# A two-layer gated cross-attention kernel: where weights are inspected and where ternary weights are made

## The chip, the core and the metric

The kernel runs on one core of a Trainium2 chip. The metric is the device time of one execution in microseconds (us); the time before is the median of three executions. TensorE is called PE, VectorE DVE, ScalarE ACT, GpSimd POOL; SyncE (SP) issues most of the DMAs.

## What is computed

Eight sequences of 100 tokens with 512 features pass through two layers. Each layer attends to a context of 722 rows and then applies a feed-forward network; both are added to the tokens through a tanh gate. Reduced to what matters:

```python
x = x + tanh(g_xattn[0]) * attn0(layernorm(x), ctx, ctx, mask)     # 16 heads of 32
x = x + tanh(g_ffn[0])   * ffn0(layernorm(x))
x = x + tanh(g_xattn[1]) * (attn1(layernorm(x), ctx, ctx) @ Wo.T + bo)
x = x + tanh(g_ffn[1])   * ffn1(layernorm(x))

# ffn0: w1, w2 [2048,512], h1, h2 [2048,2048], w3 [512,2048] drawn from -1, 0, 1; one scale a row
h = silu(x @ w1.T * s1) * (x @ w2.T * s2)
h = gelu(h @ h1.T * t1);  h = gelu(h @ h2.T * t2);  y = h @ w3.T * s3

# ffn1: weights are made ternary, activations are rounded to 8 bits
wq = clip(round(w / mean(abs(w))), -1, 1) * mean(abs(w))
aq(x) = clip(round(x * 127 / max(abs(x))), -128, 127) * max(abs(x)) / 127
y = (silu(aq(x) @ gate_q.T) * (aq(x) @ up_q.T)) -> aq -> @ down_q.T
```

## The kernel before

`flow` (line 45 onward) writes the whole program once, and every engine executes its instructions in the order in which they are written (`ORDERED`, line 21). SP's list is its DMAs: one that has to wait holds all SP DMAs behind it. `flow` is written twice: a short path that splits activations of the first feed-forward into two parts, hi and lo, in the fp32r format (the weights then have to be exact in it), and a general path that runs only if the inspected weights were not. `verdict` holds the outcome. With these inputs the short path alone runs.

**First attention.** `attention` (237) runs 8 batches of 4 units; a unit (b, oc) is four heads. In a unit, PE makes scores of the first half of the keys, then of the second half; DVE adds the mask and takes maxima; ACT makes exponentials. After the second half the hook `between0` (820) is called, then `settle` (360) finishes the unit before: six turns (PE transposes of probabilities into two PSUM buffers, evicted in turn by DVE and ACT to pT), then the product with the values. Between these pieces `take` pulls matmuls from a filler: the k and v projections of the next batch (`projections`, 156), whose k is evicted by ACT and whose v by DVE. A batch's filler runs in the order k, v, k, v, about one to a unit. At the start of a batch `load_ctx` (150) orders the first part of the context two batches ahead, in the middle the second part; three buffers hold parts. At oc = 1 `mask_bias` (786) orders the next batch's mask from SP and converts it on DVE.

`between0` also advances `inspections` (539) three times a call. A step loads 128x1024 weights by a POOL DMA; POOL takes the low 16 bits of each and adds them up. There are 88 steps.

**First feed-forward** (`feed_forward`, 463). It is run in two halves of 400 tokens (`hf` 0 and 1). There are 8 blocks of w1 and w2, 16 of h1, 16 of h2 and 4 of w3, each 1 MB and 32 matmuls. `block` (426) orders one by a POOL DMA into the pool `wts`, which has four 1 MB buffers for all large weights; a buffer is held until its last reader in program order. After a block come gelu and hi on ACT and lo on DVE (`split`, 431). In half 0, layer h1 carries `mean_weights` (578): twelve 1 MB loads of w_gate, w_up and w_down on SP and 24 Abs on ACT with accumulated sums, from which come a mean and its inverse. Layer h2 carries side work: in half 0 the normalisation and transposition of the second tokens, in half 1 the queries of the second attention (`second_queries`, 881), which load wq and keep it for the second attention. Both call `ln_rstd` (109), which has POOL raise to the power -0.5 (line 115). In half 1, `make_room` (888) orders ctxT, wk and wv ahead of w3. A w3 tile holds 128 output columns and comes by four DMAs of 256 KB.

**Second attention** (hook `between1`, 961). The same units, without a mask. `quantise_weights` (602) advances once a call: a 1 MB load on SP, then on POOL multiply and add, subtract and max with -1, min with 1, and a cast to fp8. The last batch's filler is the second feed-forward for batches 0 to 6: `hidden_rows`, `quantised_hidden` (694; on POOL, line 705 multiply and add, line 706 subtract and min) and `down_rows`; batch 7 follows with DVE in POOL's place.

Of the kernel before, what the change touches and what calls it, by code (L numbers as in the profile page):

```python
# [9 lines left out]
F32 = mybir.dt.float32  # L10
# [33 lines left out]
def flow(tc: tile.TileContext, a: dict, out: bass.AP, verdict):  # L44
# [378 lines left out]
    WT = F32R if short else F32  # L423
    COST = TH / 2400 * (1 if short else 4) + 0.016

    def block(src, shape, name):
        w = wts.tile(shape, WT, tag="w", name=name)
        nc.gpsimd.dma_start(w, src)  # L428
        return w

# [32 lines left out]
    def feed_forward(hf, xs, sets, early_work, side_work, before_down, after_down):  # L463

        everything = slice(0, TH)
# [8 lines left out]
        for op in range(HC // 2):  # L474
            w = block(a["w12"][op], [P, 2, 2, KC, P], "w12")
# [20 lines left out]
        for layer, m in enumerate(("h1", "h2")):  # L496
            outs = []
            for oc in range(HC):
                w = block(a[m + "_w"][oc], [P, HC, P], m)
# [9 lines left out]
                next((early_work, side_work)[layer], None)  # L509
                yield COST  # L510
            h = outs
            for _ in (early_work, side_work)[layer]:
                pass
# [3 lines left out]
        for oc in range(KC):  # L517
            w = wts.tile([P, HC // KC, KC, P], WT, tag="w", name="w3")
            for q in range(HC // KC):
                nc.gpsimd.dma_start(w[:, q], a["w3_w"][q][:, :, oc * P : (oc + 1) * P])  # L520
            acc = ps_sc.tile([P, 512], F32, tag="sc", name="ps_w3")
            yield from product(acc, w.rearrange("p q c o -> p (q c) o"), h)
            nc.scalar.activation(yT[oc], acc[:, :TH], AF.Identity, scale=s3g[:, oc : oc + 1])
            yield COST
        after_down()
        for i in range(BH):
            pt = ps_t.tile([P, 512], F32, tag="pst", name="ps_y")
            for oc in range(KC):
                nc.tensor.transpose(
                    pt[:S, oc * P : (oc + 1) * P], yT[oc][:, i * S : (i + 1) * S], ident  # L530
                )
            yield 0.34
            b = hf * BH + i
            nc.vector.tensor_add(x[:, b, :], x[:, b, :], pt[:S, :])
            ln_stats(b)
# [3 lines left out]
    def inspections():  # L539
        blocks = [a["w12"][i].rearrange("p a b c d -> p (a b c d)") for i in range(HC // 2)]  # L540
        blocks += [a[m][i].rearrange("p a b -> p (a b)") for m in ("h1_w", "h2_w") for i in range(HC)]
        blocks += [a["w3_w"][i].rearrange("p a b -> p (a b)") for i in range(HC // KC)]
        n = HID // 2
        blocks = [src[:, h * n : (h + 1) * n] for src in blocks for h in range(2)]
        home = rooms["seen"]
        seen = home.tile([P, n], I32, tag="seen", name="seen")
        part = home.tile([P, n], I32, tag="part", name="part")
        nc.gpsimd.memset(seen, 0)

        def fetch(src):  # L550
            w = home.tile([P, n], F32, tag="w_seen", name="w_seen", bufs=2)
            nc.gpsimd.dma_start(w, src)
            return w

        w_next = fetch(blocks[0])
        for i in range(len(blocks)):
            w = w_next
            if i + 1 < len(blocks):
                w_next = fetch(blocks[i + 1])
            low = w.bitcast(U16).rearrange("p (n two) -> p n two", two=2)[:, :, 0]  # L560
            nc.gpsimd.tensor_copy(part, low)  # L561
            nc.gpsimd.tensor_tensor(seen, seen, part, ALU.add)  # L562
            yield
        worst = small.tile([P, 1], F32, tag="worst", name="worst")
        nc.vector.reduce_max(worst, seen, axis=AX.X)
        pt = ps_t.tile([P, 512], F32, tag="pst", name="ps_seen")
        nc.tensor.transpose(pt[:1, :P], worst, ident)
        most = small.tile([1, 1], F32, tag="most", name="most")
        nc.vector.reduce_max(most, pt[:1, :P], axis=AX.X)
        nc.vector.tensor_scalar_min(verdict, most, 1.0)  # L570
        yield

# [3 lines left out]
    def mean_weights():  # L578

        for name in ("w_gate", "w_up", "w_down"):  # L580
            sums8 = small.tile([P, 8], F32, tag="w_sums", name="w_sums")
            for q in range(4):
                w = weights(a[name][q], [P, HID], name)
                yield
                for h in range(2):
                    cols = slice(h * HID // 2, (h + 1) * HID // 2)
                    i = 2 * q + h
                    nc.scalar.activation(
                        w[:, cols], w[:, cols], AF.Abs, accum_out=sums8[:, i : i + 1]
                    )  # L590
            yield
            row = small.tile([P, 1], F32, tag="w_row", name="w_row")
            nc.vector.reduce_sum(row, sums8, axis=AX.X)
# [6 lines left out]
            quant[name] = mean, inv  # L600

    def quantise_weights():

        for name in ("w_gate", "w_up", "w_down"):
            wq = rooms["q"].tile([P, 4, HID], FP8, tag=name, name=name + "_q")
            quant[name] += (wq,)
            for q in range(4):
# [481 lines left out]
```

## Time and profile before

| what | value |
|---|---|
| median of three executions | 1929.3 us (1926.24 to 1939.88) |
| the profiled execution, its time | 1932.18 us |
| its span, first to last instruction | 1930.4 us |
| first attention's batches begin (ctxT DMA behind the previous filler) | 93.3, 152.4, 216.1, 280.3, 344.8, 413.1, 475.6 us |
| first feed-forward, half 0 and half 1, to the second attention | from 621 us, to about 1240 us |
| mean granted PE clock | 0.962 |
| DMA | 204.78 MB, mean 106 GB/s |

In the page, busy times are shares of the span, and a row of 40 digits shows each engine's busy tenths in 40 slices of 48 us. In the timeline a row gives start, duration, engine, line, operation, output<-input and count, and in brackets the idle time ahead of it with what ended it. A record of SPq is a DMA issue. Matmul durations overlap: the distance of starts (0.181 us for 400 columns) is the rate.

### The profile page before, as it was taken

What the parts mean: (1) busy time and instruction counts of PE and PEld (TensorE: products, weight loads), DVE (VectorE), ACT (ScalarE), POOL (GpSimd) and SP (SyncE); (2) the same over time, 40 slices, a digit from 0 to 9 for tenths busy, and PEclk for the clock granted to TensorE, in tenths of its full rate; (3) what the DMA queues carried; (4) which work ended last, traced back from release to release, by engine and by line L of the source; (5) the groups of instructions that cost most, each with busy time, mean ns of one, the idle gap of its engine ahead of it and who ended that gap; (6) DMA issues with size and microseconds to landing.
All of it is one profiled execution on the core that took longest, in us unless ns stands there. A gap on an engine that the chain in (4) does not pass through costs nothing. (4 is left out here: it accounts for less than half of the span.)

```text
span 1930.4 us, 27472 instructions
## 1 busy us (share of the span) xinstructions
PE 1758.0 (91%) x11227; PEld 1209.7 (63%) x11227; DVE 772.7 (40%) x2180; ACT 586.1 (30%) x1187; POOL 683.7 (35%) x459
## 2 busy tenths in 40 slices
PE   5999999999979998799999896799999999998785
PEld 2555555555545988799999896655555545554453
DVE  2345455545554400110410110244444455456664
ACT  0043333343334343221322111033433333433431
POOL 0689999970030000102000001147767600003143
PEclk8999999999999998899999998899999999998898
DMA  4354454441021467457555445411122101000000
GB/s 150 128 181 158 143 168 145 144 135 38 16 77 45 168 247 261 153 175 178 170 176 175 140 144 149 103 59 61 59 83 75 54 15 32 1 1 1 9 10 19
DMA packets 67039, 204.78 MB, mean 106 GB/s; under 512 B 6408, under 2 KB 39176, under 8 KB 52340
## 3 DMA queue, kind: packets, MB, share of 16 engines
q0 software_dynamic: 41088, 138.42, 22.5%
q1 hardware_dynamic: 25816, 64.51, 10.1%
q8 instruction: 90, 1.47, 0.3%
q14 instruction: 45, 0.37, 0.1%
HBM read 201.28 MB, written 1.64 MB: 105 GB/s over the span
## 5 line engine op out<-in xcount | busy, mean ns | idle before, releaser
L453 PE MATMUL ps_h<-hi,h 128*128 128x400 f32 x1024 | 363.3, 355 | 27.0 <-DMA h<-in_h_w 27.0
L191 PE MATMUL ps_v<-wv,ctxT 128*128 128x512 f32 (+1 forms) x768 | 387.2, 612 | 0.0
L171 PE MATMUL ps_k<-ctxT,wk 128*128 128x338 f32 (+1 forms) x1024 | 364.1, 483 | 22.6 <-ACT kT L179 14.8
L453 PE MATMUL ps_h<-lo,h 128*128 128x400 f32 x1024 | 360.1, 352 | 0.0
L275 ACT ACTIVATE p<-p,negm 100x722 f32<-100x722 f32 x256 | 229.4, 896 | 244.5 <-DVE negm L272 243.8
L290 PEld LDWEIGHTS ps_pT<-ident,p 100*128 100x128 f32 (+1 forms) x1536 | 169.6, 139 | 192.4 <-issue 76.6
L171 PEld LDWEIGHTS ps_k<-ctxT,wk 128*128 128x128 f32 x1024 | 179.3, 193 | 124.0 <-issue 37.0
L290 PE MATMUL ps_pT<-ident,p 100*128 100x100 f32 (+1 forms) x1536 | 197.6, 253 | 43.2 <-DVE pT L293 21.3
L453 PEld LDWEIGHTS ps_h<-hi,h 128*128 128x128 f32 x1024 | 197.9, 193 | 29.5 <-DMA h<-in_h_w 22.1
L562 POOL TENSOR_TENSOR seen<-seen,part 128x1024 int32<-128x1024 int32 x88 | 209.4, 2379 | 7.5
L434 DVE TENSOR_TENSOR lo<-g,hi 128x400 fp32r<-128x400 f32 x96 | 55.3, 576 | 389.1 <-ACT hi L433 389.1
L453 PEld LDWEIGHTS ps_h<-lo,h 128*128 128x128 f32 x1024 | 197.8, 193 | 0.7
L191 PEld LDWEIGHTS ps_v<-wv,ctxT 128*128 128x128 f32 (+1 forms) x768 | 123.5, 186 | 97.7 <-issue 93.9
L179 ACT ACTIVATE kT<-ps_k,bk 128x384 f32<-128x384 f32 (+1 forms) x128 | 71.8, 562 | 320.2 <-PE ps_k L171 318.3
L293 DVE COPY pT<-ps_pT 128x400 f32<-128x400 f32 x180 | 102.6, 572 | 165.2 <-PE ps_pT L290 165.0
L428 POOL DMA_DIRECT2D h<-in_h_w x64 | 34.0, 532 | 360.1 <-PE ps_h L453 297.5
L115 POOL TENSOR_TENSOR ln_r<-ln_v,root 100x1 f32<-100x1 f32 (+1 forms) x14 | 10.7, 762 | 411.0 <-DVE ln_v L113 411.0
L258 DVE CUSTOM_DVE_ANT_0 p<-sc,mask 100x361 f32<-100x361 f32 x256 | 121.4, 530 | 64.0 <-PE sc L249 64.0
L258 DVE CUSTOM_DVE_ANT_0 p<-sc,zero 100x361 f32<-100x361 f32 x256 | 121.7, 530 | 57.9 <-PE sc L249 57.7
L295 ACT COPY pT<-ps_pT 128x400 f32<-128x400 f32 (+1 forms) x204 | 99.0, 487 | 113.0 <-PE ps_pT L290 112.5
L503 ACT ACTIVATE g<-ps_h,h_s 128x400 f32<-128x400 f32 x64 | 38.0, 594 | 313.3 <-PE ps_h L453 313.3
L561 POOL CAST part<-w_seen 128x1024 int32<-128x1024 uint16 x88 | 92.0, 1046 | 20.9 <-DMA w_seen<-in_h_w 12.0
(166 smaller groups left out, 2079.8 us busy)
## 6 DMA issues: line engine op xcount, KB each, us to landing
h<-in_h_w POOLq DMA_DIRECT2D x64, 1024.0 KB, 5.1
w_seen<-in_h_w POOLq DMA_DIRECT2D x64, 512.0 KB, 3.8
w<-in_w POOLq DMA_DIRECT2D x16, 1024.0 KB, 5.1
ctxT<-in_ctxT SPq DMA_DIRECT2D x16, 768.0 KB
ctxT<-in_ctxT SPq DMA_DIRECT2D x16, 676.0 KB
w_seen<-in_w POOLq DMA_DIRECT2D x16, 512.0 KB, 3.9
w_gate<-in_w_gate SPq DMA_DIRECT2D x8, 1024.0 KB
w_up<-in_w_up SPq DMA_DIRECT2D x8, 1024.0 KB
```

What stands on the lines that cost most here:

```text
L171: nc.tensor.matmul(ps[:, :kn], wk[:, c, oc * P : (oc + 1) * P], cT[:, c, :kn], start=(c == 0), stop=(c == KC - 1),)
L179: nc.scalar.activation(kT[:, oc, k0 : k0 + kn], ps[:, :kn], AF.Identity, bias=bk[:, oc : oc + 1],)
L191: nc.tensor.matmul(ps[:rn, :], cT[:, c, r0 - k0 : r0 - k0 + rn], wv[:, c, :], start=(c == 0), stop=(c == KC - 1),)
L258: nc.vector.tensor_tensor_reduce(ps[j][:, cols], sc[j][:S, :HALF], bias[:, cols], 1.0, LOWEST, ALU.add, ALU.max, m2[:, j, h : h + 1],)
L275: nc.scalar.activation(ps[j], ps[j], AF.Exp, bias=negm[:, j : j + 1], accum_out=sums[:, 4 * oc + j : 4 * oc + j + 1],)
L290: nc.tensor.transpose(pt[:kn, j, :], ps[j][:, k0 : k0 + kn], ident[:S, :S])
L293: nc.vector.tensor_copy(sb[:kn], pt[:kn])
L295: nc.scalar.copy(sb[:kn], pt[:kn])
L434: nc.vector.tensor_sub(two[1][:, cols], src, two[0][:, cols].bitcast(F32))
L453: nc.tensor.matmul(acc[:, :TH], w[:, c, :], part, start=(c == 0 and k == 0), stop=(c == len(ins) - 1 and k == len(two) - 1),)
L561: nc.gpsimd.tensor_copy(part, low)
L562: nc.gpsimd.tensor_tensor(seen, seen, part, ALU.add)
```

## The change

1. `inspections` is gone. In half 0 of the first feed-forward, `block` loads a raw copy by SP, POOL copies it to fp32r, and DVE ORs the raw bits into `seen` in four instructions of 512 columns. `judge` masks the low 12 bits after the half and sets `verdict`. Half 1 loads as before.
2. `mean_weights` is gone. `quantise_weights` runs in the first attention, six steps to a call of `between0`. Its data come in 72 stages of 128x342 (24 to a matrix), twice: once for Abs on ACT, once for the four POOL operations, after which SP stores the fp8 stage to DRAM. Two buffers hold stages. At (6, 3) what is left of it is drained. The second attention loads the three results at (0, 0) (`fetch_quantised`).
3. w3 comes in four blocks of 512 input rows, each contiguous, into four PSUM accumulators at once.
4. wq of the second attention is dropped after its first use and loaded again after the first feed-forward; wv is ordered after w3.
5. `quantised_hidden` no longer clips at 127 in its second operation.

```diff
+    LOOKS = 4
...
-    def block(src, shape, name):
-        w = wts.tile(shape, WT, tag="w", name=name)
-        nc.gpsimd.dma_start(w, src)
+    def block(src, shape, name, seen):
+
+
+        if seen is None:
+            w = wts.tile(shape, WT, tag="w", name=name)
+            nc.gpsimd.dma_start(w, src)
+            return w
+        raw = wts.tile(shape, F32, tag="w", name=name)
+        nc.sync.dma_start(raw, src)
+        w = wts.tile(shape, F32R, tag="w", name=name + "_r")
+        axes = " ".join("abcd"[: len(shape) - 1])
+        flat = f"p {axes} -> p ({axes})"
+        nc.gpsimd.tensor_copy(w.rearrange(flat), raw.rearrange(flat))
+        bits = raw.bitcast(I32).rearrange(flat)
+        n = HID // LOOKS
+        for i in range(LOOKS):
+            nc.vector.tensor_tensor(seen, seen, bits[:, i * n : (i + 1) * n], ALU.bitwise_or)
         return w
+
+    def judge(seen):
+
+        nc.vector.tensor_scalar(seen, seen, 0xFFF, None, ALU.bitwise_and)
+        worst = small.tile([P, 1], F32, tag="worst", name="worst")
+        nc.vector.reduce_max(worst, seen, axis=AX.X)
+        pt = ps_t.tile([P, 512], F32, tag="pst", name="ps_seen")
+        nc.tensor.transpose(pt[:1, :P], worst, ident)
+        most = small.tile([1, 1], F32, tag="most", name="most")
+        nc.vector.reduce_max(most, pt[:1, :P], axis=AX.X)
+        nc.vector.tensor_scalar_min(verdict, most, 1.0)
 
...
+        seen = None
+        if short and hf == 0:
+            seen = sets[0](0).tile([P, HID // LOOKS], I32, tag="seen", name="seen")
+            nc.vector.memset(seen, 0)
...
-            w = block(a["w12"][op], [P, 2, 2, KC, P], "w12")
+            w = block(a["w12"][op], [P, 2, 2, KC, P], "w12", seen)
...
-                next((early_work, side_work)[layer], None)
+                if layer == 1:
+                    next(side_work, None)
                 yield COST
-            for _ in (early_work, side_work)[layer]:
-                pass
+        for _ in side_work:
+            pass
...
-        for oc in range(KC):
-            w = wts.tile([P, HC // KC, KC, P], WT, tag="w", name="w3")
-            for q in range(HC // KC):
-                nc.gpsimd.dma_start(w[:, q], a["w3_w"][q][:, :, oc * P : (oc + 1) * P])
-            acc = ps_sc.tile([P, 512], F32, tag="sc", name="ps_w3")
-            yield from product(acc, w.rearrange("p q c o -> p (q c) o"), h)
-            nc.scalar.activation(yT[oc], acc[:, :TH], AF.Identity, scale=s3g[:, oc : oc + 1])
-            yield COST
+        acc = [ps_sc.tile([P, 512], F32, tag="sc", name="ps_w3") for _ in range(KC)]
+        for q in range(HC // KC):
+            w = block(a["w3_w"][q], [P, KC, D], "w3", seen)
+            for oc in range(KC):
+                cols = slice(oc * P, (oc + 1) * P)
+                for c in range(KC):
+                    for k, part in enumerate(h[q * KC + c]):
+                        first = q == 0 and c == 0 and k == 0
+                        last = q * KC + c == HC - 1 and k == len(h[0]) - 1
+                        nc.tensor.matmul(
+                            acc[oc][:, :TH], w[:, c, cols], part, start=first, stop=last
+                        )
+                        yield COST
+                if q == HC // KC - 1:
+                    nc.scalar.activation(
+                        yT[oc], acc[oc][:, :TH], AF.Identity, scale=s3g[:, oc : oc + 1]
+                    )
         after_down()
+        if seen is not None:
+            judge(seen)
...
-    def inspections():
...
-            low = w.bitcast(U16).rearrange("p (n two) -> p n two", two=2)[:, :, 0]
-            nc.gpsimd.tensor_copy(part, low)
-            nc.gpsimd.tensor_tensor(seen, seen, part, ALU.add)
-            yield
...
-    def mean_weights():
-
...
+    STAGE = 342
+
+    def stages(name):
+
+        where = [(q, c0, min(STAGE, HID - c0)) for q in range(4) for c0 in range(0, HID, STAGE)]
+
+        def fetch(i):
+            q, c0, n = where[i]
+            t = xts.tile([P, STAGE], F32, tag=f"xc{i % 2}", name="w_stage")
+            nc.sync.dma_start(t[:, :n], a[name][q][:, c0 : c0 + n])
+            return t[:, :n], i, q, slice(c0, c0 + n)
+
+        coming = fetch(0)
+        for i in range(len(where)):
+            now = coming
+            if i + 1 < len(where):
+                coming = fetch(i + 1)
+            yield now
+
...
+    def quantise_weights():
+
+
+        for name in NAMES:
+            n = 4 * -(-HID // STAGE)
+            sums = small.tile([P, n], F32, tag="w_sums", name="w_sums")
+            for w, i, q, cols in stages(name):
+                nc.scalar.activation(w, w, AF.Abs, accum_out=sums[:, i : i + 1])
                 yield
-                for h in range(2):
-                    cols = slice(h * HID // 2, (h + 1) * HID // 2)
-                    i = 2 * q + h
-                    nc.scalar.activation(
-                        w[:, cols], w[:, cols], AF.Abs, accum_out=sums8[:, i : i + 1]
-                    )
             row = small.tile([P, 1], F32, tag="w_row", name="w_row")
...
-    def quantise_weights():
-
-        for name in ("w_gate", "w_up", "w_down"):
...
-            for q in range(4):
-                w = weights(a[name][q], [P, HID], name)
-                yield
-                nc.gpsimd.tensor_scalar(w, w, quant[name][1], MAGIC, ALU.mult, ALU.add)
-                nc.gpsimd.tensor_scalar(w, w, MAGIC, -1.0, ALU.subtract, ALU.max)
-                nc.gpsimd.tensor_scalar_min(w, w, 1.0)
-                nc.gpsimd.tensor_copy(wq[:, q, :], w, saturate=False)
-
-        mg, mu, md = (quant[name][0] for name in ("w_gate", "w_up", "w_down"))
+            wq = dram.tile([P, 4, HID], FP8, tag=name, name=name + "_dram")
+            quant[name] = mean, inv, wq
+
...
+        for name in NAMES:
+            _, inv, wq = quant[name]
+            for w, i, q, cols in stages(name):
+                nc.gpsimd.tensor_scalar(w, w, inv, MAGIC, ALU.mult, ALU.add)
+                nc.gpsimd.tensor_scalar(w, w, MAGIC, -1.0, ALU.subtract, ALU.max)
+                nc.gpsimd.tensor_scalar_min(w, w, 1.0)
+                t = xts.tile([P, STAGE], FP8, tag=f"xc{2 + i % 2}", name="wq_stage")
+                t = t[:, : cols.stop - cols.start]
+                nc.gpsimd.tensor_copy(t, w, saturate=False)
+                nc.sync.dma_start(wq[:, q, cols], t)
+                yield
+
+    def fetch_quantised():
+        for name in NAMES:
+            t = rooms["q"].tile([P, 4, HID], FP8, tag=name, name=name + "_q")
+            nc.sync.dma_start(t, quant[name][2])
+            quant[name] = quant[name][:2] + (t,)
...
-        engine.tensor_scalar(hq, h, MAGIC, 127.0, ALU.subtract, ALU.min)
+        engine.tensor_scalar(hq, h, MAGIC, None, ALU.subtract)
...
-        for _ in range(3):
-            next(inspected, None)
+        for _ in range(6):
+            next(quantised, None)
         if oc == 1 and b + 1 < B:
...
         if (b, oc) == (B - 2, KC - 1):
+            for _ in quantised:
+                pass
...
-        second["q"] = wq, bq
+        second["bq"] = bq
...
         second["wk"] = weights(a["L1_Wk"], [P, KC, D], "wk1")
+
+    def make_more_room():
         second["wv"] = weights(a["L1_Wv"], [P, KC, D], "wv1")
-
-    def make_more_room():
...
+    second["wq"] = weights(a["L1_Wq"], [P, KC, D], "wq1")
     wo = weights(a["L1_Wo"], [P, KC, D], "wo1")
...
-            for _ in queries(1, *second["q"], turned_room(), second["qT"][1]):
+            for _ in queries(1, second["wq"], second["bq"], turned_room(), second["qT"][1]):
                 take(0.7)
             output_bias()
+            fetch_quantised()
             return
-        next(quantised, None)
```

## The prediction

> **What bounds the kernel now.** I read the page's busy shares and slices first. TensorE (PE) is busy 91% of the span. GpSimd (POOL) is full in slices 2 to 8, the first attention, where it inspects weights.
>
> ```profile
> PE 1758.0 (91%) x11227; PEld 1209.7 (63%) x11227; DVE 772.7 (40%) x2180; ACT 586.1 (30%) x1187; POOL 683.7 (35%) x459
> PE   5999999999979998799999896799999999998785
> POOL 0689999970030000102000001147767600003143
> ```
>
> So a cost matters where it stops PE, and a gain is only what PE waits for today. The PE timeline gives those waits. The worst are at the end of the second feed-forward half, where w3 tiles come through one buffer:
>
> ```profile
> 1194.30 0.67 PE L453 MATMUL ps_w<-hi,w 128*128 128x400 f32 x1 [11.98 <-DMA w<-in_w_w]
> 1206.75 0.45 PE L453 MATMUL ps_w<-hi,w 128*128 128x400 f32 x1 [3.67 <-DMA w<-in_w_w]
> 1218.04 0.70 PE L453 MATMUL ps_w<-hi,w 128*128 128x400 f32 x1 [3.63 <-DMA w<-in_w_w]
> 1230.55 0.45 PE L453 MATMUL ps_w<-hi,w 128*128 128x400 f32 x1 [3.62 <-DMA w<-in_w_w]
> ```
>
> An attention batch takes 62.5 us while POOL is idle (413.7 to 476.2 us) and 64.6 while it inspects (280.8 to 345.4). The feed-forward runs 32 matmuls to a block in 5.81 us (the spacing of POOL's block DMAs).
>
> **Gains.** (1) w3. Before, wq, wk and wv hold three of the four weight buffers; after, wq is dropped and reloaded and wv loads later, so three buffers serve w3, in contiguous blocks. The waits above sum to 22.9 us. From 1194.30 to the first ps_y at 1238.05 is 43.75 us; less three waits 32.9, where four blocks should take 23.3: 9.6 us lost to a slow clock after each wait (granted 0.66 to 0.84 there). Of 32.5 I count **-31**.
>
> (2) The first half's stalls. Without the means' 12 MB and sums on the way, PE loses waits of 2.8 + 3.0 + 2.9 us for h blocks and 1.9 + 2.0 + 2.0 for the mean's row: 14.6. At 805 PE waits 10.2 us, since POOL's DMA issues stand behind its pow (ln_r, L115). That block's first 17 matmuls then come 0.333 us apart rather than 0.181: 2.6 more. After, the loads go through SP, and only POOL's copy stands behind the pow: pow 1.0, copy 1.9, DVE's lead 2.2, about 5 left of 12.8. Sum 14.6 + 7.8, rounded down: **-20**. The same stall in the second half (8.2 us at 1080) stays.
>
> (3) The tail. The clip at 127 goes from hq on POOL:
>
> ```profile
> 1804.14 7.08 POOL L706 TENSOR_SCALAR hq<-hid 100x2048 bf16<-100x2048 f32 x1
> 1811.30 0.56 POOL L115 TENSOR_TENSOR ln_r<-ln_v,root 100x1 f32<-100x1 f32 x1
> 1817.26 1.52 PE L249 MATMUL sc<-kT,xa 32*100 32x361 f32 x2 [8.16 <-DVE m L258]
> 1911.03 1.51 PE L716 MATMUL ps_hq<-ident_bf,hq 100*128 100x100 bf16 x16 [9.00 <-POOLq L1017]
> ```
>
> A lone subtract has no row. Multiply and add takes 1.97 us, a lone min 5.37: bounds 1.9 and 5.4; I take 1.97, as it too has no min. That is 5.1 us off each. PE waits for it twice (through the pow at 1811, and directly at 1911), and once POOL holds up L352 (3.67 us against 0.75): **-11** (-3 at 5.4). (4) No inspection: 2.1 us for each of batches 0 to 2; batches 3 to 5 have POOL busy again: **-6**. The second attention has PE full while POOL quantises (1280 to 1480): freeing POOL there is 0. Gains: 68.
>
> **Costs in the first attention, phase A.** The means are now 72 stages of 128x342 (175 KB), six at each call of the hook, calls 1 to 12 (batches 0 to 2). Each is an Abs on ACT, which waits for its SP DMA through two buffers. Abs of 1024 took 1.05 us and 0.19 for the accumulator; I take 0.5 + 0.19. Landing: 1 MB took 5.1 us, 512 KB 3.8, so a line gives 2.9 for 175 KB. A rule of the Trainium skill bears on it (DMA: Bandwidth & Descriptors, section "Anatomy of one DMA": some 2.0 us fixed, plus the size over 436 GB/s): 2.4. Two stages have landed when a group starts; each further pair waits for a buffer, an issue and a landing, 3.7 us from start to start. Six take 0.69 x 2 + 2 waits of 3 us + 0.69 x 2 = about 8.8 us of ACT's time (7.8 by the rule; 6 us less in all). Behind them on ACT stand exponentials and pT copies, and PE turns wait for these:
>
> ```profile
> 159.56 0.58 ACT L179 ACTIVATE kT<-ps_k,bk 128x384 f32<-128x384 f32 x1 [2.99 <-PE ps_k L171]
> 160.18 0.90 ACT L275 ACTIVATE p<-p,negm 100x722 f32<-100x722 f32 x1
> 161.62 0.49 ACT L295 COPY pT<-ps_pT 128x400 f32<-128x400 f32 x1 [0.45 <-PE ps_pT L290]
> ```
>
> The group falls between the first two lines. ACT is free at 160.1, so the group ends at 168.9, the exponential at 170.0, the pT copy at 170.5. PE's fourth turn needs that buffer and came at 163.7: 6.8 us. That holds in units filled with k projections (ACT evicts up to the hook), two of four per batch. In v units ACT has nothing for some 9 us before the hook, which hides the group; there the mask's DMA comes about 1 us late. Three batches: 6 x 6.8 + 3, and half of the 2.6 us restart each: **+52** (20 to 65).
>
> **Phase B.** Stages 0 to 71 of quantising run in batches 3 to 5: four POOL operations, then a store. At 2048 columns they take:
>
> ```profile
> 1275.58 1.98 POOL L610 TENSOR_SCALAR w_gate<-w_gate,w_gate_i 128x2048 f32<-128x2048 f32 x1 [24.45 <-issue]
> 1277.65 7.09 POOL L611 TENSOR_SCALAR w_gate<-w_gate 128x2048 f32<-128x2048 f32 x1
> 1284.83 5.37 POOL L612 TENSOR_SCALAR w_gate<-w_gate 128x2048 f32<-128x2048 f32 x1
> 1290.26 1.89 POOL L613 CAST w_gate_q<-w_gate 128x2048 fp8e4<-128x2048 f32 x1
> ```
>
> 16.3 us over 6 is 2.7; about 0.15 fixed per operation and gaps of 0.08 add 0.8: **3.5 us** a stage (3.2 to 3.8), 252 in all. The Trainium skill (GPSIMD Engine Reference, section 4.1 "Engine selection") calls one-input elementwise work on GpSimd roughly line-rate. By it all four would cost as the cast, 0.42 us each: 1.8 with gaps, and phase B would hide. The rows with max and min, at 7.09 and 5.37, speak against it; I use the rows.
>
> POOL itself keeps nobody waiting, but SP does. SP issues in program order: the store waits for POOL's cast, and the next batch's mask stands behind twelve stores. SP is held to PE anyway:
>
> ```profile
> 280.26 0.54 SPq L153 DMA_DIRECT2D ctxT<-in_ctxT  x1
> 280.85 0.54 SPq L791 DMA_DIRECT2D mask<-in_mask  x1
> ```
>
> The ctxT load waits for the end of a batch's projections (S); today the mask follows at once, and DVE casts it 25.6 us later (153.0 against 178.0 for batch 1). After, in batch 3: two issues and a landing (3.5) + 12 x 3.5 + 2.9 = 48.4 after S. DVE stands 22.8 us at the cast; behind it are the evictions of turns and so PE, which runs on for 3 us at most: 20. Then SP waits at the second ctxT load, 33.4 us after S, which slips with PE; POOL runs dry there for about 8 us. So a batch takes 24 x 3.5 + 8 = 92 us in place of 64: 28 in each of batches 4 and 5. The mask of batch 7 is in time, 25 us into batch 6. Sum **+76** (40 to 95). What would be late next, ctxT, has half a batch of slack.
>
> **Costs in the first feed-forward half.** A block is now loaded raw by SP, copied by POOL, ORed into `seen` by DVE, and holds two of four buffers. The loop: after block i-1 ends, gelu, hi and lo take 1.9 us (DVE reaches the ORs behind lo), four ORs of 512 at 0.69 + 0.03 (L329's undisturbed duration) 2.9, then SP loads block i+2 (5.2 from issue to use, as for w_gate at 1270.40), POOL copies 1.9, with 0.3 of semaphores: 12.2 us against two blocks, 11.6. So 0.3 a block x 44 = 13; I take **+12**. If the copy meets the ORs (L329 reached 2.0 beside a busy POOL), up to 1.3 a block, 57; if the DMA lands in 4.5, 0. judge() puts a mask, a maximum and a transpose ahead of ps_y: **+2**.
>
> **Edits at nothing.** The second attention's hook now issues three 1 MB loads of ternary weights on SP at (0, 0), ahead of the next ctxT: the first reader of the weights is batch 7's filler, and ctxT has half a batch (31 us) to come; without that cover some 15 us, once. The reloaded wq gets the buffer of w3's third block, lands 5.2 us later while the fourth (5.8) still runs, and is read after it; without that cover 5. wv stands behind w3's second block, 11.6 us ahead of the end. The twelve 1 MB loads that leave the second attention kept only POOL waiting, and the 24 Abs that leave the first feed-forward half ran on an ACT that waits for PE there. On the DMA engines 44 MB of inspection (share 0.46 in a batch) give way to 24 MB of stages and 3 MB of stores.
>
> **Sum.** -31 - 20 - 11 - 6 + 52 + 76 + 12 + 2 = +74. The profiled span is 1930.4 us (1932.2 with what lies around it), 3 us above the median of 1929.3; so 2004 to 2006 for the profiled run and **2003** for the median.
>
> **Rivals.** *POOL keeps up* (not slower): if a stage takes 1.85 us or less, twelve come before DVE reaches the mask (3.5 + 12 x 1.85 + 2.9 = 28.6, the 25.6 and 3 us of PE's run-ahead). Then phase B is 0: 1927; if ACT's groups are also half hidden, 1900. For it: the rule above, and POOL off the critical path today. Against: rows L611, L612. *Contention in the feed-forward*: ORs and copies collide, +45 more: 2048. For it: L329 and L352 stretch beside POOL; against: a longer period pulls them apart. *w3 still starves*, the freed buffers going elsewhere: +31, 2034. Against: wq's last reader comes seven blocks earlier.
>
> **Chances.** My case 0.58, POOL keeps up 0.24 (half of it by over 1% faster), contention 0.13, w3 starves 0.05. My case with its bounds spans 1950 to 2040. With the others the range is 1905 to 2055. A measurement here tells about 1% from no change: faster by over 1% 0.13, within 1% 0.14, slower 0.73.
>
> **What would show it.** Right: SP standing on POOL's cast in batches 3 to 5, DVE idle some 20 us before the mask's cast, those batches near 90 us; ACT idle inside Abs groups; w3 without waits; hq near 2 us. Wrong: POOL stages under 2.5 us, masks issued ahead of stores, or feed-forward blocks above 6.3 us.

## The result and the profile after

The changed kernel takes **2084.2 us** (median of four, 2080.9 to 2090.7) where the kernel before takes 1932.7 in the same rounds: a ratio of 1.079 (95% interval 1.074 to 1.084). The prediction, 2003 us with a range of 1905 to 2055, had the direction, and missed the size by 81 us. The profiled span is 2082.4 us, 152.0 above that of before.

Against the predicted sum of +74, by stages, between the same events in both traces (the x += of each batch's end, L352; the first w12 matmul; the first ps_y of each half):

| stretch | predicted | measured |
|---|---|---|
| batches 0 to 2 (phase A, less the inspection) | +46 | +73 |
| batches 3 to 5 (phase B) | +76 | +124 |
| batches 6 and 7 | 0 | -9 |
| first feed-forward, half 0 (-20 + 12 + 2) | -6 | +5 |
| half 1 (w3) | -31 | -34 |
| second attention and tail | -11 | -7 |
| sum | +74 | +152 |

The page of the changed kernel gives the same picture: PE's busy share falls from 91% to 85%, and the holes lie in the first attention's slices.

```profile
PE 1774.3 (85%) x11227; PEld 1207.4 (58%) x11227; DVE 915.4 (44%) x2358; ACT 594.9 (29%) x1283; POOL 424.6 (20%) x410
PE   5968888491927998898999998999999999998786
POOL 0000001778676201233231000000000000001222
PEclk8978999795968999999999999999999999998898
```

In slices 8, 10 and 12, PE has 4, 1 and 2 tenths. DVE's timeline of the changed kernel says what it stood at: the first three lines are the mask's cast in batches 3 to 5, with the idle time ahead of it, and the fourth is PE's next turn behind the first of them.

```profile
407.90 0.54 DVE L821 CAST mask<-mask 100x722 f32<-100x722 int32 x1 [28.27 <-DMA mask<-in_mask]
519.77 0.54 DVE L821 CAST mask<-mask 100x722 f32<-100x722 int32 x1 [46.80 <-DMA mask<-in_mask]
633.80 0.54 DVE L821 CAST mask<-mask 100x722 f32<-100x722 int32 x1 [48.58 <-DMA mask<-in_mask]
410.55 0.93 PE L290 MATMUL ps_pT<-ident,p 100*128 100x100 f32 x4 [28.02 <-DVE pT L293]
```

Before, the cast in batch 3 did not wait:

```profile
307.33 0.72 DVE L792 CAST mask<-mask 100x722 f32<-100x722 int32 x1
```

DVE's three waits sum to 123.7 us, all of phase B's loss. PE waited 28.02 us behind the first of them: the 3 us of run-ahead that the prediction gave PE did not exist. SP's queue in batch 3 shows what holds the mask, and what comes behind it (lines left out are marked `...`):

```profile
352.90 0.55 SPq L153 DMA_DIRECT2D ctxT<-in_ctxT  x1
353.55 1.05 SPq L593 DMA_DIRECT2D w_stage<-in_w_gate  x2
362.12 0.33 SPq L643 DMA_DIRECT2D w_gate_dram<-wq_stage  x1
...
403.88 0.33 SPq L643 DMA_DIRECT2D w_gate_dram<-wq_stage  x1
404.30 0.32 SPq L820 DMA_DIRECT2D mask<-in_mask  x1
417.17 0.56 SPq L153 DMA_DIRECT2D ctxT<-in_ctxT  x1
```

The mask goes out behind the twelfth store, 51.4 us after the batch began (3.5 + 12 x 3.5 = 45.5 by the prediction's numbers). Then SP stands for 12.9 us at the next ctxT load, since PE, released by this very mask, has not yet reached the middle of the batch. POOL's stages were predicted well (3.5 us): below is one line for each of the four operations of the first stage, and the next stage starts 3.70 us after it.

```profile
358.38 0.57 POOL L637 TENSOR_SCALAR w_stage<-w_stage,w_gate_i 128x342 f32<-128x342 f32 x1 [294.55 <-DMA w_stage<-in_w_gate]
359.03 1.37 POOL L638 TENSOR_SCALAR w_stage<-w_stage 128x342 f32<-128x342 f32 x1
360.49 1.07 POOL L639 TENSOR_SCALAR w_stage<-w_stage 128x342 f32<-128x342 f32 x1
361.63 0.47 POOL L642 CAST wq_stage<-w_stage 128x342 fp8e4<-128x342 f32 x1
362.08 0.56 POOL L637 TENSOR_SCALAR w_stage<-w_stage,w_gate_i 128x342 f32<-128x342 f32 x1
```

In phase A, ACT's timeline of the first group of six Abs (the filler's k eviction ahead of it, an exponential behind it) has the predicted shape: two landings in the middle, 7.4 us in all where 8.8 were predicted. A stage ordered at 100.25 is used at 102.76, one ordered at 112.12 at 115.35: 2.5 and 3.2 us, about the line's 2.9. The 2.4 that the prediction drew from the Trainium skill (DMA: Bandwidth & Descriptors, section "Anatomy of one DMA") is near, but that section gives its fit for DMAs ordered from GpSimd, and these come from SP.

```profile
99.17 0.58 ACT L179 ACTIVATE kT<-ps_k,bk 128x384 f32<-128x384 f32 x1 [2.99 <-PE ps_k L171]
99.65 0.48 ACT L615 ACTIVATE w_stage<-w_stage 128x342 f32<-128x342 f32 x1
...
102.76 0.49 ACT L615 ACTIVATE w_stage<-w_stage 128x342 f32<-128x342 f32 x1 [2.07 <-DMA w_stage<-in_w_gate]
...
106.13 0.49 ACT L615 ACTIVATE w_stage<-w_stage 128x342 f32<-128x342 f32 x1 [2.32 <-DMA w_stage<-in_w_gate]
...
107.08 0.88 ACT L275 ACTIVATE p<-p,negm 100x722 f32<-100x722 f32 x1
```

The windows view prices phase A (batches 0 to 2: length, busy time of each engine, granted clock, DMA share, GB/s). The first line is the changed kernel:

```profile
92.90:352.90 260.00, 207.57 (x1275) 112.49 (x1275) 92.65 (x291) 105.85 (x294) 0.00 (x0) 0.88 0.26 74
```

and this one the kernel before:

```profile
93.30:280.30 187.00, 181.52 (x1279) 99.15 (x1280) 97.96 (x288) 70.64 (x150) 172.63 (x132) 1.00 0.48 158
```

Of the 73 us more, PE is busy for 26 more with the same matmuls: the granted clock is 0.88 where it was 1.00. The other 47 are idle, and PE's own list of waits in that stretch says behind what. After:

```profile
PE ps_pT L290 <- ACT pT L295: 39.7, 9, 9.4
PE ps_pT L290 <- DVE pT L293: 8.3, 3, 2.9
PE ps_v L191 <- ACT kT L179: 4.1, 1, 4.1
```

Before:

```profile
PE ps_pT L290 <- ACT pT L295: 4.2, 2, 2.7
PE ps_pT L290 <- DVE pT L293: 1.3, 2, 0.9
```

So 39.6 us more are spent behind ACT, where the groups of Abs stand, and 7.0 more behind DVE. DVE itself stood 22.8 us at three masks there (16.89, 2.81 and 3.13), but most of that did not reach PE.

The tail's waits shrank little, from 8.16 to 6.33 us and from 9.00 to 7.28, since the subtract alone still takes 5.36 us:

```profile
1958.27 5.36 POOL L737 TENSOR_SCALAR hq<-hid 100x2048 bf16<-100x2048 f32 x1
1969.56 1.52 PE L249 MATMUL sc<-kT,xa 32*100 32x361 f32 x2 [6.33 <-DVE m L258]
2063.94 1.51 PE L747 MATMUL ps_hq<-ident_bf,hq 100*128 100x100 bf16 x16 [7.28 <-POOLq L1043]
```

PE's list of waits has no load of w3 in the second half any more (22.9 us before).

### The profile page after: what moved, and what is told of

It reads as the page before. It is cut to its first block, busy times and chain, and to the rows that moved or that the text cites. A ratio compares the mean times of both kernels' runs of the same rounds, so it can differ in the third digit from the quotient of the medians.

```text
span 2082.4 us, 28129 instructions
## 1 busy us (share of the span) xinstructions
PE 1774.3 (85%) x11227; PEld 1207.4 (58%) x11227; DVE 915.4 (44%) x2358; ACT 594.9 (29%) x1283; POOL 424.6 (20%) x410
## 5 line engine op out<-in xcount | busy, mean ns | idle before, releaser
L191 PE MATMUL ps_v<-wv,ctxT 128*128 128x512 f32 (+1 forms) x768 | 397.9, 626 | 4.1 <-ACT kT L179 4.1
L171 PE MATMUL ps_k<-ctxT,wk 128*128 128x338 f32 (+1 forms) x1024 | 371.5, 491 | 22.8 <-ACT kT L179 15.0
L290 PE MATMUL ps_pT<-ident,p 100*128 100x100 f32 (+1 forms) x1536 | 207.9, 262 | 194.6 <-DVE pT L293 142.0
L479 PE MATMUL ps_h<-hi,h_r 128*128 128x400 f32 x512 | 180.0, 352 | 21.6 <-POOL h_r L439 21.6
L479 PE MATMUL ps_h<-hi,h 128*128 128x400 f32 x512 | 180.2, 352 | 8.2 <-DMA h<-in_h_w 8.2
L479 PE MATMUL ps_h<-lo,h 128*128 128x400 f32 x512 | 178.1, 348 | 0.0
L479 PE MATMUL ps_h<-lo,h_r 128*128 128x400 f32 x512 | 177.9, 347 | 0.0
L443 DVE TENSOR_TENSOR seen<-seen,h 128x512 int32<-128x512 int32 x128 | 115.7, 904 | 3.3
L479 PEld LDWEIGHTS ps_h<-hi,h_r 128*128 128x128 f32 x512 | 97.3, 190 | 27.0 <-POOL h_r L439 27.0
L479 PEld LDWEIGHTS ps_h<-hi,h 128*128 128x128 f32 x512 | 97.3, 190 | 9.1 <-DMA h<-in_h_w 8.5
```

Of the source, the lines that this page charges most:

```text
L171: nc.tensor.matmul(ps[:, :kn], wk[:, c, oc * P : (oc + 1) * P], cT[:, c, :kn], start=(c == 0), stop=(c == KC - 1),)
L191: nc.tensor.matmul(ps[:rn, :], cT[:, c, r0 - k0 : r0 - k0 + rn], wv[:, c, :], start=(c == 0), stop=(c == KC - 1),)
L290: nc.tensor.transpose(pt[:kn, j, :], ps[j][:, k0 : k0 + kn], ident[:S, :S])
L443: nc.vector.tensor_tensor(seen, seen, bits[:, i * n : (i + 1) * n], ALU.bitwise_or)
L479: nc.tensor.matmul(acc[:, :TH], w[:, c, :], part, start=(c == 0 and k == 0), stop=(c == len(ins) - 1 and k == len(two) - 1),)
```

## The experiments

The theory after the result: the weights' work is short enough to be hidden, and nearly all of its 197 us in the first attention comes from *order*: the mask and ctxT behind stores on SP, Abs in groups ahead of pT copies on ACT. The rivals: the work itself is too much (POOL's long operations, DMA traffic), or it slows its neighbours through shared resources. For e1 to e4 the time is that of one execution, beside one of 1925.2 us for the kernel before; for the others it is the median of four, beside 1931 to 1934 us.

**e1: the mask ahead of the stages.** Only the mask's DMA moves, to the call before.

```diff
+        if oc == 0 and b + 1 < B:
+            later["mask"] = mask_load(b + 1)
         for _ in range(6):
             next(quantised, None)
         if oc == 1 and b + 1 < B:
-            biases[b + 1] = mask_bias(b + 1)
+            biases[b + 1] = mask_bias(b + 1, later["mask"])
```

> The changed kernel, with the next mask's DMA ordered at oc = 0 ahead of that call's six stages (its conversion on DVE stays at oc = 1). Nothing is left out. Order theory (the first attention's loss in batches 3 to 5 is the mask standing behind stores on SP, seen as DVE waits of 28, 47 and 49 us): the wait of batch 3 vanishes, and those of batches 4 and 5 shrink, because SP itself reaches a batch's start only every 24 x 3.64 us + 6 = 93 us while PE needs 64: waits of about 7, 30 and 29 us at the conversions in batches 4, 5 and 6, 66 in place of 124; the mask waits of 17 + 3 + 3 us in batches 0 to 2 go too. Time about 2015 us. Rival (POOL's work and the small transfers slow PE, ACT and DVE by contention, and the mask waits are only where the lag shows): PE gets no further, the lag shows up at another wait, and the time stays within 15 us of 2084.

Measured 2037.2 us. Phase A fell by 15 (its mask waits went), batch 3 has no wait and takes 62.5 us, but batches 4 to 6 wait 19.6, 36.4 and 38.7 us, 94.7 in all:

```profile
DVE mask L824 <- DMA mask<-in_mask: 94.7, 3, 38.7
```

As the theory said, SP arrives late at the batch's beginning itself, so a mask ordered there is late too: the wait isn't removed but comes one batch later. It is longer than the 66 us expected, since SP begins its batches 100 to 104 us apart, not 93.

**e2: shorter stages.** The subtract with max and the min make way for one multiply and add; the clip of the ternary weights to -1 and 1 is left out.

```diff
-                nc.gpsimd.tensor_scalar(w, w, MAGIC, -1.0, ALU.subtract, ALU.max)
-                nc.gpsimd.tensor_scalar_min(w, w, 1.0)
+                nc.gpsimd.tensor_scalar(w, w, 1.0, -MAGIC, ALU.mult, ALU.add)
```

> The changed kernel with POOL's two clipping operations (subtract and max, min) replaced by one multiply and add; the clipping of the ternary weights to -1 and 1 is left out. POOL work for a stage falls from 3.46 to 1.6 us, DMAs and SP order unchanged. Order theory: SP's distance between stores is then set by the store, the next fetch and its landing, about 5.6 us for two stages, 2.8 each rather than 3.64, so the masks are 12 x 0.84 = 10 us earlier in batch 3 and a batch takes about 92 us rather than 112: mask waits near 17, 28 and 28 us, 73 in place of 124; time about 2033 us. If only POOL's rate counted (no landing in the loop), stages of 1.9 us and waits under 5 us each: 1970. Rival (contention by transfers): no change beyond 15 us, since the transfers stay.

Measured 2009.9 us; the mask waits of batches 3 to 5 are 13.7, 16.8 and 20.9, 51.4 in all (73 expected). L638 takes 0.48 us where the two operations took 2.44. So the stage's length does set the wait, and the operations with max and min make most of that length. Whether a clip can be had for less was not tried.

**e3: one step after each turn.** The six steps are spread over settle's six turns.

```diff
             for c in range(NK):
                 got.append(turn(ps0, c, vector))
                 take(0.74)
+                if layer == 0:
+                    next(quantised, None)
...
-        for _ in range(6):
-            next(quantised, None)
```

> The changed kernel with the six steps of a call taken one after each of the six turns of settle, not in one group ahead of it. Nothing is left out. Theory for batches 0 to 2 (+73 us over the kernel before): ACT stands in a group of six Abs with two landings inside, ahead of the copies that PE's turns wait for, and PE's clock drops after each wait (PE busy 208 us for 182 us of work). With single steps no Abs should wait much over 1 us: batches 0 to 2 fall by about 50 us. The mask at oc = 1 then stands behind six stages fewer, so batch 3's wait falls to about 3 us and the next two to about 30 each: 64 in place of 124. Together about 1975 us. Rival (it is the amount of ACT work and of transfers): batches 0 to 2 stay within 15 us of what they took.

Measured 2000.1 us. Phase A's loss went from 73 to 14 us, as the x += of batch 2 shows (316.3 us; 375.4 with the groups; 302.4 before): 59 where 50 were expected, for the same 72 Abs. ACT's waits for stages fell from 66 to 16 us, PE's waits in phase A from 52.4 to 12.5, and PE's granted clock there was 0.97. Phase B gave back some of it, with 94.5 us of mask waits where 64 were expected.

**e4: no ORs.** The inspection's four ORs are left out.

> The changed kernel without the four ORs of a block: the inspection of the weights is left out (raw load by SP and POOL's copy to fp32r stay). First feed-forward half, 303.7 us in the changed kernel. Theory (the loop lo, four ORs, load of the block after next, copy sets the pace, 6.6 us a block on average against 5.81, and ORs beside a copy stretch from 0.69 to over 2 us): without ORs the raw buffer is free at the copy's end, blocks come every 5.81 us, the half takes about 275 us: 2055 us in all. Rival (POOL's copy and the two-deep buffers alone set the pace): the half stays above 295 us.

Measured 2052.9 us, 31 less; half 0 took 270 us in place of 304. So the ORs cost about 31 us; without them PE waits for POOL's copies only once, 4.9 us. That the ORs alone are at fault does not follow, since e12 keeps them.

**e5: w3 and wq alone**, on the kernel before (parts 3 and 4 of the change). **e6: with it hq** as two operations:

```diff
-        engine.tensor_scalar(hq, h, MAGIC, 127.0, ALU.subtract, ALU.min)
+        engine.tensor_scalar(hq, h, 1.0, -MAGIC, ALU.mult, ALU.add)
```

**e7: with both, the variance add early.** `ln_rstd` is cut in two: DVE's add of the variance is issued at h1's block 8, POOL's pow stays at the start of h2.

```diff
-        for later["xs"] in normalised(1, HI_LO[1]):
+        v = ln_var(BH, B)
+        yield
+        for later["xs"] in normalised(1, HI_LO[1], v):
...
+                if (layer, oc) == (0, 8):
+                    next(side_work)
```

> The kernel before with parts 3 and 4 alone: w3 in four blocks of rows, wq loaded again after the first feed-forward, wv ordered after w3. Theory (the gain of the second half is the w3 stalls alone, and it does not depend on the moved inspection): first matmul of the half to first sc falls by about 33 us, 1932 to about 1899. Rival (part of the 34 us came from POOL and the DMA engines being free of other parts of the change, or the reloaded wq is late without them): a gain of 20 or less, 1912 or more.

> The run with w3 by rows, and hq made on POOL as multiply by 1 and add -MAGIC (two operations, without the clip at 127, as in the change) in place of a lone subtract. Theory (POOL's price goes by the operation: multiply and add 1.97 us, lone subtract 5.36, subtract and min 7.08): hq takes about 1.97 us, both waits of the tail (8.2 and 9.0 us) shrink by about 5, and the time falls by 11 to 14 us, to about 1886. Rival (a second operation always costs, so that only the missing min counts): hq stays at 5.4 and the gain is about 7, 1892.

> The run with w3 and hq, and the variance add for the tokens turned in layer h2 issued on DVE 8 blocks of h1 earlier, so that POOL's pow does not wait on DVE's queue and POOL's DMA issues behind it go out in time. Theory (in both halves PE's stalls at the start of h2, 10.2 and 8.2 us with about 2.6 us of slow clock behind each, come from POOL's issues standing behind the pow): about 20 us less, to about 1865. Rival (the stalls come from the loads themselves being late): no change, about 1886.

Measured 1899.7, 1886.4 and 1861.1 us beside 1933.6 for before: ratios 0.983 (0.979 to 0.986), 0.976 (0.972 to 0.979) and 0.964 (0.960 to 0.969). All three theories hold. In e6, hq takes 1.90 us on POOL:

```profile
L715 POOL TENSOR_SCALAR hq<-hid x7: 1897/1897/1898, 1723.1 to 1862.3; 100x2048 bf16<-100x2048 f32 x7
```

So for 2048 columns multiply and add took 1.90 us, a lone subtract 5.36, and subtract with min 7.08. In e7, PE's waits for h loads fall from e6's 26.7 us to 8.5, and the slow clock behind the two long ones goes with them.

**e8: all masks early.** Six buffers, all masks ordered in batches 0 to 2; stages as in the change.

```diff
-    masks = pool(left, "masks", 2)
+    masks = pool(left, "masks", 6)
...
+    AHEAD = {(0, 0): 2, (0, 1): 3, (0, 2): 4, (1, 2): 5, (2, 0): 6, (2, 2): 7}
...
+        if (b, oc) in AHEAD:
+            mask_load(AHEAD[b, oc])
```

> The changed kernel with all masks ordered from SP in batches 0 to 2 into six buffers, so that no mask stands behind stores in batches 3 to 5; the conversions stay where they are. Theory (phase B costs 124 us only because the mask's DMA stands behind twelve stores on SP; the next thing late is ctxT in batches 5 and 6, since 72 stages of 3.64 us are 262 us against three batches of 64): mask waits 0, about 20 us of ctxT waits and 6 us from POOL beside DVE, 2084 to about 1985. Rival (POOL's work slows the first attention by itself, through shared SBUF access or the DMA of stages): batches 3 to 5 stay above 75 us each, 2020 or more.

Measured 1993.0 us, ratio 1.031 (1.028 to 1.035). No mask wait is left, and batches 3 and 4, in which nothing waits, take 62.5 us with POOL busy for 87 and 82% of them (x += at 358.81, 421.37, 483.78), as fast as one with POOL idle before. That refutes the rival: in these batches POOL's work and its DMAs cost nothing that shows. What remains in batches 5 and 6 is order again: twice ctxT behind stores, seen at PE (34.5 us, where 20 were expected), and once the tokens' pow behind POOL's last stages, seen at DVE.

```profile
543.97 6.40 PE L171 MATMUL ps_k<-ctxT,wk 128*128 128x384 f32 x12 [17.17 <-DMA ctxT<-in_ctxT]
596.36 4.78 PE L171 MATMUL ps_k<-ctxT,wk 128*128 128x338 f32 x10 [17.37 <-DMA ctxT<-in_ctxT]
```

```profile
640.11 0.16 DVE L117 TENSOR_TENSOR ln_u<-ln_r 100x4 f32<-100x4 f32 x1 [20.06 <-POOL ln_r L115]
```

The pow's wait was not foreseen: the stages end at 639.1, behind the point at which the program wants the first feed-forward's tokens.

**e9: the work where it is covered.** Spread as in e3, masks early, hq as in e6, and the two halves of the work interleaved, so that POOL has three stages (10.9 us) in a unit of 15.6, in buffers of their own.

```diff
+        yield from means("w_gate")
+        for step, mean_of in (("w_gate", "w_up"), ("w_up", "w_down")):
+            made = ternary(step)
+            for _ in means(mean_of):
+                yield
+                next(made)
+                yield
...
+        yield from ternary("w_down")
```

**e10: with the variance early**, as in e7. **e11: as e10, no inspection** in half 0.

> The changed kernel with the first attention's work put where it is covered: one step after each of settle's turns as in e3, w_gate's quantising interleaved with w_up's means and w_up's with w_down's (three POOL stages and three Abs to a unit, own buffers for POOL's raw stages), masks early as in e8, hq as multiply and add. POOL then has 3 stages of 3.64 us, 10.9 us, in a unit of 15.6. Theory (both phases cost only through order and crowding, the work itself fits): phase B 124 becomes 0, phase A 73 becomes about 15, hq -7, so 2084 to about 1895. Rival (SP in order: each Abs load now stands behind a store that waits for POOL, and ACT waits for it in front of pT copies): 48 Abs at 1 us and more, 1935 or above.

> The interleaved kernel with the variance add 8 blocks earlier in both halves. Theory (the stall at the start of h2 comes from what stands behind POOL's pow; in half 0 the copies, in half 1 the block loads): about 11 us in half 1 and 4 to 7 in half 0, so 15 to 18 us less than e9, near 1880. Rival (in half 0 the copies are late anyway through the ORs): 10 to 11 less, near 1885.

> The same without the inspection in the first feed-forward: half 0 loads its blocks as half 1 does, with no raw copy, no POOL copy and no OR; what the kernel would check of the weights is left out. Theory (the ORs, stretched beside POOL's copy, set the pace of half 0, as leaving them out gave 33 us): about 33 us less than e10, near 1847, and no better than the before kernel with the w3, hq and variance edits (1861) by more than its own 14 us of mean and inspection waits. Rival (with the pow out of the way the copies and ORs fit in the block time): 10 us or less.

Measured 1892.1, 1880.4 and 1848.8 us: ratios 0.979 (0.975 to 0.982), 0.973 (0.970 to 0.977) and 0.957 (0.954 to 0.961). In e9 the eighth batch's x += is at 650.1 us where before has 636.3 and the changed kernel 827.7: 191 us of loss have become 14, with every one of the 144 steps still done. e9 makes all the changes of order at once; what interleaving gives alone was not tried. e10 gives 12 us by the medians where 15 to 18 were expected, nearer to its rival's 10 to 11. In the traces half 0 (the memset of `seen` to the first ps_y) falls from 303.1 to 296.9 us and half 1 (first ps_y to first ps_y) from 283.7 to 273.4, 16 together, as the theory had it; but that is one pair of executions, and e9's was the slowest of its four. e11 puts the inspection at 32 us.

**e12: the copy on ACT.** In half 0 the raw block is copied by ACT in place of POOL, and ordered one block ahead.

```diff
-        nc.gpsimd.tensor_copy(w.rearrange(flat), raw.rearrange(flat))
+        nc.scalar.copy(w.rearrange(flat), raw.rearrange(flat))
...
+            while order and len(coming) < 2:
+                coming.append(block(*order.pop(0), seen))
+            return coming.pop(0)
```

> The interleaved kernel with the variance early, and in half 0 the raw block copied to fp32r by ACT in place of POOL, each block ordered, copied and ORed one block ahead of its matmuls (so that ACT's copy stands ahead of the previous block's gelu instead of behind it). All of the computation is there. Theory (the 31 us of inspecting come from DVE's ORs and POOL's copies stretching each other while both stand on the way to the next block): the ORs take 0.69 us each (four 2.9, in 5.8 us of a block), PE's waits on the copy (22 us) go, and the time is near that without inspection plus judge, about 1853. Rival (raw and copy holding two of four buffers sets the pace, whoever copies): blocks stay above 6.2 us, 1872 or more. A third outcome: ACT's copies of about 2 us delay gelu and hi, and PE waits there, 1860 to 1880.

Measured **1849.8 us**, ratio 0.957 (0.955 to 0.960), the fastest version that does all of the computation, and within 1 us of e11, which leaves the inspection out. The row of the h blocks' ORs (minimum, median and maximum in ns) is this in the changed kernel:

```profile
L443 DVE TENSOR_TENSOR seen<-seen,h x128: 676/692/2402, 876.3 to 1085.1; 128x512 int32<-128x512 int32 x128
```

and this in e12:

```profile
L450 DVE TENSOR_TENSOR seen<-seen,h x128: 681/692/694, 683.5 to 866.2; 128x512 int32<-128x512 int32 x128
```

The medians are equal; the ORs of up to 2.4 us are gone. The Trainium skill (SBUF — State Buffer, section "SBUF: two separate sides") says that DVE operations with two SBUF inputs and a GpSimd operation exclude each other on a shared port pair, for the whole instruction. By it an OR that meets a copy takes, as an estimate from these rows, up to 0.69 plus the copy's 1.9, 2.6 us; the maximum of 2.40 agrees, and so do the 694 ns at most beside ACT's copies of 1.91 us. e12 changed two things, the copy's engine and its place, so the rows show that the stretching went with POOL's copy; how the 31 us divide between the two was not tried.

## Why the prediction was wrong

The measured change is 78 us above the predicted sum. Phase B makes 48 of that, phase A 27 and half 0 of the first feed-forward 11; the other stretches give back 9.

**Phase B: the failed step.** "POOL runs dry there for about 8 us. So a batch takes 24 x 3.5 + 8 = 92 us in place of 64: 28 in each of batches 4 and 5." The mechanism, mask behind stores behind POOL, was right, and so nearly was the stage (3.7 us from start to start). The batch took 112 to 113 us, from the ctxT loads' issues at 352.90, 464.92, 577.58 and 690.92. 24 x 3.7 is 89, so POOL was dry for some 23 us. The 8 us are SP's wait at the second ctxT load alone, from a PE that is nearly there (33.4 + 20 after the batch's start, less 45.5 for the mask's issue, is 7.9). That wait was 12.9, and POOL's were longer still, since the mask closes a loop: SP's mask, landing 3.6, DVE's conversion 2.7, PE's rest of the half batch 6.6, then SP's ctxT load at last and, after it, POOL's next data, another 6. POOL's timeline has both waits:

```profile
423.25 0.56 POOL L637 TENSOR_SCALAR w_stage<-w_stage,w_gate_i 128x342 f32<-128x342 f32 x1 [15.72 <-DMA w_stage<-in_w_gate]
471.06 0.56 POOL L637 TENSOR_SCALAR w_stage<-w_stage,w_up_i 128x342 f32<-128x342 f32 x1 [6.58 <-DVE v L199]
```

The first is this loop in the middle of the batch, the second stands at the beginning of the next. A loop through SP, DVE and PE has to be walked to the end and back to its start before a period is given. The rest of phase B's miss is the run-ahead of 3 us that was not there, and the first mask, 6 us later than worked out. e1 and e8 show that the order makes this loss: with the mask alone out of the way, batch 3 takes 62.5 us.

**Phase A: right in place, two terms mis-sized.** "Half of the 2.6 us restart each" made 8 us of clock; it was 26, since the granted clock was 0.88 over all three batches. The masks, "about 1 us late", were to cost 3 and cost PE 7. The groups' 6 x 6.8 = 41 us came out at 39.6, in part by luck. In batches 1 and 2 PE's long waits lie in the k units alone, as said, but take 4.6 to 5.5 us each. In batch 0 it waits in all four units (4.1, 4.4, 9.4 and 4.3), the longest time behind an Abs whose stage load stood behind a ctxT load on SP, 11.9 us on ACT. The remedies tell the terms apart: e1, without mask waits there, gave back 15 us of the 73, and e3, which has none either and spreads the steps, 59.

**Half 0: the gains right, the contention rival in part.** PE's 24.7 us of waits for h blocks and for the means' rows are gone, and of the stall behind the pow 4.9 us are left ("about 5"). The cost is the mis-sized term. The forecast took +12 for the loop and put 57 on a meeting of ORs and copies at every block; PE waits 24.8 us more for POOL's copies, and 3.1 at the half's start for an eviction behind ORs on DVE. In about half of the blocks one of the four ORs is stretched to some 2.2 us. "Against: a longer period pulls them apart" was half true. By the runs the whole inspection costs 31 to 32 us (e4, e11).

**Right:** w3 -34 for -31 (e5: 34 alone, so the gain was w3's, and the stages moved elsewhere took no part in it).

**hq:** the bound of 5.4 was the right one, not the 1.97 taken "as it too has no min". Of the -7 in the last stretch only 2.7 lie behind the second attention's last x +=, near the -3 given for that bound. Another 4.3 lie in the batch after its third x +=, and the prediction had put them at nothing ("freeing POOL there is 0"): before, POOL quantised until 1531 us, not 1480, that x += took 3.17 us beside it, where 0.75 is usual, and PE waited 5.5 us behind DVE in the batch, 1.4 after. So the -7 is near -11 partly by luck.

**Missed:** batches 6 and 7, -9: the inspections of before still ended in batch 6, with PE waits of 5.4 us for DVE and 1.8 for their verdict that are gone after; by the x += of batch 6, 6.7 of the 9 fall there. One reading has a slip: 153.0 to 178.0 is 25.0 us; the 25.6 that the sum uses count from the ctxT load at 152.4.

The range failed at phase B: its upper end of 95 us came from a longer stage, and every case held POOL's dry time at 8 us, so none had the mask's delay fed back through SP.

## What to carry to other kernels

When work is put under cover of another engine, look first at the in-order queue that feeds it, here SP's DMAs: a store that waits for a slow engine holds every load behind it, and such loads release the engine that SP waits for next. Read the cost of a wait at the engine that sets the pace: DVE stood 22.8 us at masks in phase A, PE only 8.3 behind DVE. Spread the steps, order the small loads far ahead, and match the slow engine's work to the unit (10.9 us in 15.6): with all three, the same work went from 191 us to 14. Before giving work to POOL, ask of the row's exact operation, and which two-input DVE work it will meet.

## What the runs showed of the hardware

- On POOL, for 2048 columns of fp32, multiply and add took 1.90 us, a lone subtract 5.36, a lone min 5.37, subtract with max or min 7.1. Multiplying by 1 and adding -c in place of a lone subtract of c was 2.8 times as fast; a lone add was not tried.
- DVE's two-input OR of 512 columns took 0.69 us beside ACT's copies and up to 2.40 beside POOL's.
- Short waits cost twice: in phase A, with waits of up to 9.4 us, PE was idle for 47 us more and ran 26 us longer on the same matmuls, at a granted clock of 0.88 where it was 1.00 before. With the steps spread (e3) it was 0.97.
